# A two-layer graph attention kernel: shorter lookahead and dropped buffers for the gathered rows, four pairs of weighted rows, completing products in three parts

## The chip, the core and the metric

The kernel runs on one core of one Trainium2 chip. The metric is the device time of one execution in microseconds (us); of several runs the median counts. The engines are named as in the profile: PE is TensorE (PEld its weight loads), DVE is VectorE, ACT is ScalarE, POOL is GpSimd, SP is the engine from which most plain DMAs are issued. "SPq" or "POOLq" is an engine's instruction queue.

## What is computed

A graph of 6250 nodes and 100,000 edges, sorted by destination, plus a loop at every node. Two attention layers and a small network are added to x:

```python
def gat_conv(x, src, dst, W, a_src, a_dst, bias, heads):
    n = x.shape[0]
    h = (x @ W).reshape(n, heads, -1)
    alpha_s = (h * a_src[None]).sum(-1)
    alpha_d = (h * a_dst[None]).sum(-1)
    e = jax.nn.leaky_relu(alpha_s[src] + alpha_d[dst], NEG_SLOPE)
    m = jax.ops.segment_max(e, dst, num_segments=n)
    e = jnp.exp(e - m[dst])
    denom = jax.ops.segment_sum(e, dst, num_segments=n)
    alpha = e / (denom[dst] + 1e-16)
    out = jax.ops.segment_sum(h[src] * alpha[:, :, None], dst, num_segments=n)
    return out.reshape(n, -1) + bias

h = jnp.maximum(_layernorm(x, axis=-1), 0.0)
h = jax.nn.relu(gat_conv(h, src, dst, W1, a_src1, a_dst1, b1, HEADS))   # 768 -> 4 heads of 64
h = jax.nn.relu(gat_conv(h, src, dst, W2, a_src2, a_dst2, b2, 1))       # 256 -> 256
h = jax.nn.relu(h @ Wm1 + bm1)
out = x + (h @ Wm2 + bm2)
```

All numbers are float32.

## The kernel before

**Stages.** First the features of all 49 tiles of 128 nodes are computed (lines 519 to 562); each tile's row (features, ones for the denominator, powers of the scores) is kept in SBUF (`kept`) and stored to `table[1]` in memory. Then `layer_edges` runs for layer 1, and while it runs, finished node tiles go through `Node1.steps` to `table[2]`, over the place of `kept`. Then `layer_edges` runs for layer 2, and finished node tiles go through `Node2.steps` to the output.

**Edges.** The edges are cut into tiles of 128, four tiles to a group, 196 groups (NG), and two tiles to a *pair*, the unit of buffers. For every tile GpSimd issues one indirect DMA (line 663) that fetches the 128 source rows out of the table. A pair's rows land in one buffer `G` of the pool `gathered`, which has 20 buffers (line 259). In layer 1 the vector engine makes each edge's weight (lines 741 and 751) and the weighted rows `hw` (line 753) from `G`, and TensorE sums them by destination with a 0/1 matrix `hot` (line 765). In layer 2 the weight is put into the 0/1 matrix (line 748) and TensorE reads `G` itself.

**Order.** The program's order is written out by hand: `layer_edges` walks the groups, and in each group places gathers, `pair(g, 0)`, sums, masks, the steps of node tiles, `pair(g, 1)`. Each engine runs its own part of this order; semaphores join the engines. `gather(g)` is placed AHEAD = 8 groups before `pair(g, 0)`; in the last groups this distance falls to 4 (line 885). From group SHORT = NG - 28 = 168 on, `rows_in(layer, skip)` asks the pool for one more tile at some of the pairs and drops it (lines 320 and 658).

**Pairs fetched soon.** GpSimd has nothing to do in the first stage, so 23 pairs of layer 1 (list SOON) are gathered there, as soon as part of the table is stored: line 357, 46 gathers. Rows that are not there yet are taken as row 0 and masked out. These 23 buffers go to memory (`soon_away`) and come back when their group draws near (`soon_back`, line 368, on SP's queue). The missing rows are completed by a product: `soon_hits` (line 383, vector engine) makes 0/1 matrices, `soon_missing` (line 394, TensorE) multiplies them with the `kept` tiles, 2 to 20 tiles for each of the 46 edge tiles, `soon_out` (line 400, ScalarE) copies the result out of PSUM, and `soon_whole` (line 406, vector engine) adds it into `G`. With `at` the group of such a pair, the product for the first tile is placed in group at-8 and copied out in at-6, that for the second in at-5 and at-3; `soon_whole` stands in group at, before `pair(at, 1)`.

**The seam between the layers.** The first 11 edge tiles of layer 2 are gathered before the last two or three node tiles are finished (`first_rows`, line 334) and completed in the same way (lines 305 and 307).

**Buffers of `hw`.** In layer 1 the weighted rows of a pair use one of 8 buffers (line 640), in layer 2 the weighted 0/1 matrices one of 14.

Of the kernel before, what the change touches and what calls it, by code (L numbers as in the profile page):

```python
# [27 lines left out]
NT = -(-N // P)  # L28
NQ = 4 * NT
TPG = 4  # L30
NG = NQ
# [23 lines left out]
SOON_AT = {2 * g + 1: i for i, g in enumerate(SOON_GROUP)}  # L55
SOON_FROM, SOON_HELD = min(SOON), 16
BARE = 8
SHORT = NG - 28


UP_AT = {4 * u + 11: u for u in range(NU - 16)}
# [10 lines left out]
def kernel(  # L72
# [244 lines left out]
                nc.vector.tensor_tensor(first_i[layer][:, j:j + n], of, ok, ALU.mult)  # L317
                j += n

    def rows_in(layer, skip=False):  # L320

        if skip:
            gp.tile([P, 2, max(TW.values())], F32, name="G")
        return gp.tile([P, 2, max(TW.values())], F32, name="G")[:, :, :TW[layer]]

# [45 lines left out]
    def soon_sources(pool, i):  # L371

        if i < len(SOON):
            soon_of[i] = pool.tile([P, 2 * P], I32, name="soon_of", bufs=2)
            nc.sync.dma_start(soon_of[i], bcast(src_rows, 2 * P, 2 * P * soon_pair[i]))
# [12 lines left out]
    def soon_missing(k):  # L388
        if 0 <= k < 2 * len(SOON):
            there, hit = SOON[k // 2], soon_hit.pop(k)  # L390
            assert not any(T in renewed for T in range(there, NT))
            soon_p[k] = ps.tile([P, TW[1]], F32, name="missing1", tag="n")
            for T in range(there, NT):
                nc.tensor.matmul(soon_p[k], hit[:, T - there], kept[T], start=(T == there),  # L394
                                 stop=(T == NT - 1))

    def soon_out(pool, k):
        if 0 <= k < 2 * len(SOON):
# [235 lines left out]
    def layer_edges(layer, H, node, pre, matched, pre_pool):  # L634
# [2 lines left out]

        C = HID // H
        with tc.tile_pool(name=f"eg{layer}", bufs=6) as eg, \
                tc.tile_pool(name=f"hw{layer}", bufs=8 if layer == 1 else 14) as hwp, \  # L640
                tc.tile_pool(name=f"sum{layer}", bufs=4) as sums, \
                tc.tile_pool(name=f"sm{layer}", bufs=4) as sm:
            G, hot, e_ps, o_ps = {}, {}, {}, {}
# [7 lines left out]
            def gather(g):  # L651
                if not 0 <= g < NG:
                    return
                for t in tiles(g):
                    k = TPG * g + t
                    soon = layer == 1 and k // 2 in SOON_AT
                    if k // 2 not in G:
                        skip = g >= SHORT and k // 2 % (4 if g < SHORT + 9 else 2 if g < SHORT + 18 else 1) == 0
                        G[k // 2] = (soon_back(SOON_AT[k // 2], skip) if soon else
                                     first_G.get(layer, {}).get(k // 2) or rows_in(layer, skip))  # L660
                    if soon or k < FIRST + len(THERE.get(layer, ())):
                        continue
                    nc.gpsimd.indirect_dma_start(  # L663
                        out=G[k // 2][:, k % 2], out_offset=None, in_=table[layer],
                        in_offset=bass.IndirectOffsetOnAxis(ap=src_i[:, k:k + 1], axis=0))
# [66 lines left out]
            def pair(g, p):  # L732

                if 2 * p not in tiles(g):
                    return
                Gp = G.pop(TPG // 2 * g + p)
                e1, e2 = ((Gp[:, :, RW[1]:RW[1] + 4], Gp[:, :, RW[1] + 4:]) if layer == 1 else
                          (Gp[:, :, HID:HID + 1], Gp[:, :, HID + 2:]))
                at = TPG * (g % 4) + 2 * p
                rho, v, w = (e_ps[g // 4][:, at:at + 2, k * H:(k + 1) * H] for k in range(3))  # L740
                nc.vector.tensor_mul(v, e2, rho)  # L741
                if layer == 2:
                    w = sm.tile([P, 2, H], F32, name="w")
                    nc.vector.tensor_max(w, v, e1)  # L744
                    hw = hwp.tile([P, 2, P], F32, name="hw")
                    for t in range(2):
                        k = TPG * g + 2 * p + t
                        nc.vector.tensor_scalar(hw[:, t], iota_ps, dcol[:, k:k + 1], w[:, t],  # L748
                                                ALU.is_equal, ALU.mult)
                else:  # L750
                    nc.vector.tensor_max(w, v, e1)  # L751
                    hw = hwp.tile([P, 2, H, C + 1], F32, name="hw")
                    nc.vector.tensor_mul(  # L753
                        hw, Gp[:, :, :RW[1]].rearrange("p t (h c) -> p t h c", h=H),
                        w.unsqueeze(3).to_broadcast([P, 2, H, C + 1]))
                u = g // 2
                if u not in o_ps:
                    o_ps[u] = ps.tile([P, RW[layer]], F32, name="o_ps", tag="o", bufs=3)
                for t in range(2):
                    k = 2 * p + t  # L760
                    if layer == 2:
                        l, r = hw[:, t], Gp[:, t]
                    else:
                        l, r = hot[g][:, k], hw[:, t].rearrange("p h c -> p (h c)")
                    nc.tensor.matmul(o_ps[u], l, r[:, :RW[layer]], start=(g % 2 == 0 and k == 0),  # L765
                                     stop=(g % 2 == 1 and k == tiles(g)[-1]))
# [4 lines left out]
                    for _ in range(n):  # L771
                        nc.tensor.matmul(idle_ps[0], idle[:, :P], idle, start=True, stop=True)

            done, run, late, idle_ps, begun = {}, {}, [], [], {}

            def take_sum(u):

# [99 lines left out]
            for g in range(NG):  # L877
                t, j = divmod(g, 4)
                if layer == 2 and g >= NG - 2:
                    if g == NG - 2:  # L880
                        last_pairs()
                    continue
                if g == NG - 2:
                    at_end.append(g)
                while gathered < min(NG, g + 1 + min(AHEAD, max(4, SHORT - g))):
                    gather(gathered)
                    gathered += 1
                pair(g, 0)
                if g == NG - 1:
                    pair(g, 1)  # L890
                if g == NG - 2:
                    gather_up(NU - 2)
                advance(g)
                if taken_up(2 * g) is not None:
                    gather_up(taken_up(2 * g))
                if g <= NG - 4:
                    make_hot(g + 1)
                if g in (NG - 4, NG - 3):
                    make_hot(g + 2)
                if j == 0:  # L900
                    if layer == 1:
                        fetch_rows(t + 4)
                    node.prefetch(t)
                    if layer == 2 or t == 0:
                        meet(t + 1)
                    if layer == 1 and t > 0:
                        meet(t + 2)
                elif j == (2 if t < NT - 1 else 1):
                    node.ahead(t)
                elif j % 2 and (layer == 2 or t > 0):  # L910
                    make_mask((g + (11 if layer == 1 else 7)) // 2)
                if layer == 1 and t == 0:
                    for u in ((), (4, 5), (6,), (7,))[j]:
                        make_mask(u)
                    if j == 1:
                        parts_out(1)
                    if j == 2:
                        meet(2)
                if layer == 1:
                    for i, at in enumerate(SOON_GROUP):  # L920
                        for k, hits_at in ((2 * i, at - 10), (2 * i + 1, at - 6)):
                            if g == hits_at + 3 + (k % 2 == 0):
                                soon_out(sm, k)
                            if g == at:
                                soon_whole(G, k)
                            if g == hits_at:
                                soon_hits(pre_pool, k)
                            if g == hits_at + 1 + (k % 2 == 0):
                                soon_missing(k)
                        if g == at - 13:  # L930
                            soon_sources(pre_pool, i)
                if g == NG - 3:
                    idle_ps.append(ps.tile([P, 4 * P], F32, name="idle_ps", tag="parts", bufs=1))
                if g >= NG - 3:
                    stay_warm(3)
                if g < NG - 1:
                    pair(g, 1)
                advance(g, 1)
                if j == 3:
                    if layer == 1:  # L940
                        parts_out(t + 2)
                    join(t + 1)
                if taken_up(2 * g + 1) is not None:
                    gather_up(taken_up(2 * g + 1))
                if NG - 3 <= g < NG - 1:
                    stay_warm(3)
                hot.pop(g, None)
                if layer == 1 and g == NG - 6:
                    first_sources(2)
# [537 lines left out]
```

## Time and profile before

| | us |
|---|---|
| median of 5 runs | 2103.39 (2101.19 to 2106.25) |
| the profiled execution | 2098.68 |
| its span | 2096.8 |

The costliest groups that the change and the prediction touch, from the page (busy us, instructions, mean ns of one):

| line and engine | what | count | busy us | mean ns |
|---|---|---|---|---|
| L663 POOL | gathers of rows | 1507 | 1434.4 | 952 |
| L357 POOL | gathers of the pairs fetched soon | 46 | 44.4 | 964 |
| L753 DVE | weighted rows, layer 1 | 391 | 272.2 | 696 |
| L748 DVE | weighted 0/1 matrices, layer 2 | 782 | 285.0 | 406 |
| L394 PE | completing products | 1028 | 242.1 | 392 |
| L765 PE | sums by destination, layer 1 | 1564 | 454.3 | 426 |
| L765 PE | sums by destination, layer 2 | 1564 | 465.0 | 435 |
| L383 DVE | 0/1 matrices of the completing products | 46 | 75.1 | 1632 |

How to read it: a float32 product of one tile appears as two matmul rows, so 1028 rows at L394 are 514 tile products. The chain that ended last is split by the page as DMA 30%, PE 28%, DVE 18%, issue 13%, POOL 10%; it follows one releaser back at each step and changes engines often. The TensorE clock granted over the span was 0.895 of full speed.

### The profile page before, as it was taken

Reading aid. Unit: us, or ns where it says so; the run is one execution under the profiler, and the core shown is the slowest. Engines: PE = TensorE matmul, PEld = TensorE weight load, DVE = VectorE, ACT = ScalarE, POOL = GpSimd, SP = SyncE. Lnnn points to the kernel's source line nnn. Section 1 sums busy time; section 2 is a strip of 40 time slices with the busy share of each in tenths; the row PEclk is TensorE's granted clock in tenths of the full one; section 3 lists DMA queues with packets and bytes.
Section 4 is the critical chain, followed back from the end, with each engine's and each line's share of the span. In section 5 each row is a group of like instructions: output and inputs, shape, how many; then the busy total and the mean of one; then the engine's idle time right before and its main releaser. Section 6 shows DMA issues by size and latency. Waiting matters only on the chain.

```text
span 2096.8 us, 27028 instructions
## 1 busy us (share of the span) xinstructions
PE 1661.3 (79%) x7727; PEld 1201.2 (57%) x7729; DVE 1417.9 (68%) x4195; ACT 436.7 (21%) x1368; POOL 1526.9 (73%) x1666
## 2 busy tenths in 40 slices
PE   9986878887887888877777777777777777777877
PEld 6874757665665675655545554545555455454544
DVE  7856888887887888888776655555555555555554
ACT  5761111111111111111121111111111111111211
POOL 7067777777777777777777777777777777777774
PEclk9997999989999998999988888888888888888889
DMA  9999666666666666666546455555555555555553
GB/s 346 351 349 323 183 180 188 180 180 186 184 176 184 189 180 186 178 181 182 167 135 224 133 181 177 162 181 167 171 182 157 182 175 164 182 161 177 169 178 108
DMA packets 167330, 400.38 MB, mean 191 GB/s; under 512 B 36631, under 2 KB 54254, under 8 KB 167174
## 3 DMA queue, kind: packets, MB, share of 16 engines
q0 software_dynamic: 75072, 211.10, 37.2%
q1 hardware_dynamic: 90732, 185.99, 24.7%
q10 hardware_dynamic: 1370, 1.48, 0.2%
q8 instruction: 65, 1.06, 0.2%
q14 instruction: 91, 0.75, 0.1%
HBM read 333.87 MB, written 64.56 MB: 190 GB/s over the span
## 4 chain that ended last, share of the span: by engine, by line
DMA 30%; PE 28%; DVE 18%; issue 13%; POOL 10%; ACT 1%; DVEq 0%; SPq 0%; ACTq 0%; POOLq 0%
DMA G<-table,src_i 27%; PE o_ps L765 12%; POOL G L663 10%; PE y_ps L1139 7%; PE h_ps L457 5%; DVE hw L753 4%; DVE soon_hit L383 3%; DVE hot L691 2%; DVE factors L741 2%; DVE hw L748 1%; DVE factors L751 1%; PE y_ps L1078 1%; DVE mask L680 1%; DMA xTt<-in_xT 1%; PE tp L1129 1%
## 5 line engine op out<-in xcount | busy, mean ns | idle before, releaser
L663 POOL DMA_INDIRECT G<-table,src_i x1507 | 1434.4, 952 | 459.1 <-issue 333.6
L765 PE MATMUL o_ps<-G,hw 128*128 128x258 f32 x1564 | 465.0, 435 | 228.7 <-DVE hw L748 227.8
L765 PE MATMUL o_ps<-hw,hot 128*128 128x260 f32 x1564 | 454.3, 426 | 170.5 <-DVE hw L753 155.0
L765 PEld LDWEIGHTS o_ps<-G,hw 128*128 128x128 f32 x1564 | 316.0, 215 | 349.5 <-DVE hw L748 281.1
L741 DVE TENSOR_TENSOR factors<-G,factors 128x8 f32<-128x8 f32 (+1 forms) x782 | 129.2, 165 | 502.6 <-DMA G<-table,src_i 498.4
L765 PEld LDWEIGHTS o_ps<-hw,hot 128*128 128x128 f32 x1564 | 297.8, 204 | 290.5 <-DVE hw L753 222.4
L791 ACT ACTIVATE sum<-acc 32x260 f32<-32x260 f32 (+1 forms) x384 | 160.0, 417 | 1278.8 <-DVE acc L782 1248.6
L753 DVE TENSOR_TENSOR hw<-G,factors 128x520 f32<-128x520 f32 x391 | 272.2, 696 | 39.9 <-DVE factors L751 0.5
L748 DVE TENSOR_SCALAR hw<-iota_ps,dcol,w 128x128 f32<-128x128 f32 x782 | 285.0, 406 | 14.4
L394 PE MATMUL missing<-kept,soon_hit 128*128 128x268 f32 x1028 | 242.1, 392 | 0.0
L394 PEld LDWEIGHTS missing<-kept,soon_hit 128*128 128x128 f32 x1028 | 195.8, 192 | 36.0
L1139 PE MATMUL y_ps<-wm,mT 128*128 128x384 f32 x392 | 202.7, 653 | 0.0
L457 PE MATMUL h_ps<-w,r 128*128 128x264 f32 (+1 forms) x588 | 137.6, 388 | 5.5 <-ACT r L447 5.3
L691 DVE TENSOR_TENSOR hot<-iota_ps,dcol 128x512 f32<-128x512 f32 x196 | 133.6, 682 | 0.0
L457 PEld LDWEIGHTS h_ps<-w,r 128*128 128x128 f32 x588 | 108.4, 191 | 28.0 <-ACT r L447 9.0
L1139 PEld LDWEIGHTS y_ps<-wm,mT 128*128 128x128 f32 x392 | 86.9, 245 | 63.8 <-issue 41.5
L357 POOL DMA_INDIRECT G<-table,soon_i x46 | 44.4, 964 | 74.1 <-DMA xTt<-in_xT 53.9
L782 DVE SCALAR_TENSOR_TENSOR acc<-acc,keep,o_ps 128x260 f32<-128x260 f32 (+1 forms) x192 | 91.3, 476 | 1.8 <-PE o_ps L765 1.8
L751 DVE TENSOR_TENSOR factors<-factors,G 128x8 f32<-128x8 f32 x391 | 68.1, 174 | 13.6 <-DVE factors L741 0.2
L383 DVE TENSOR_TENSOR soon_hit<-soon_of,iota_ps 128x1408 f32<-128x1408 int32 (+18 forms) x46 | 75.1, 1632 | 0.0
L744 DVE TENSOR_TENSOR w<-factors,G 128x2 f32<-128x2 f32 x391 | 62.3, 159 | 13.5 <-DVE factors L741 0.2
L969 ACT ACTIVATE rT<-tp,bT 128x128 f32<-128x128 f32 x196 | 61.1, 363 | 43.3 <-PE tp L963 42.2
(418 smaller groups left out, 1201.6 us busy)
## 6 DMA issues: line engine op xcount, KB each, us to landing
xt<-in_x SPq DMA_DIRECT2D x96, 384.0 KB, 6.0
drow<-dmod_d SPq DMA_DIRECT2D x49, 512.0 KB, 5.6
mask_d<-mask SPq DMA_DIRECT2D x97, 256.0 KB, 2.9
mask<-mask_d SPq DMA_DIRECT2D x97, 256.0 KB, 4.8
G<-table,src_i POOLq DMA_INDIRECT x1507
xTt<-in_xT SPq DMA_DIRECT2D x49, 384.0 KB, 6.7
out<-y SPq DMA_DIRECT2D x48, 384.0 KB, 3.3
table<-kept SPq DMA_DIRECT2D x49, 134.0 KB, 4.6
```

Source lines behind the costliest of these rows:

```text
L383: nc.vector.tensor_tensor(soon_hit[k][:, :m], soon_of[i][:, t * P:(t + 1) * P].unsqueeze(1).to_broadcast([P, m, P]), nid_ps[:, SOON[i]:].u ...
L394: nc.tensor.matmul(soon_p[k], hit[:, T - there], kept[T], start=(T == there), stop=(T == NT - 1))
L457: nc.tensor.matmul(h_ps[:, :n], r[:, k], w1[:, k, :n], start=(k == 0), stop=(k == KI - 1))
L663: nc.gpsimd.indirect_dma_start(out=G[k // 2][:, k % 2], out_offset=None, in_=table[layer], in_offset=bass.IndirectOffsetOnAxis(ap=src_i[:, ...
L691: nc.vector.tensor_tensor(hot[g][:, T[0]:T[0] + n], iota_ps.unsqueeze(1).to_broadcast([P, n, P]), dcol[:, k:k + n].unsqueeze(2).to_broadca ...
L741: nc.vector.tensor_mul(v, e2, rho)
L748: nc.vector.tensor_scalar(hw[:, t], iota_ps, dcol[:, k:k + 1], w[:, t], ALU.is_equal, ALU.mult)
L753: nc.vector.tensor_mul(hw, Gp[:, :, :RW[1]].rearrange("p t (h c) -> p t h c", h=H), w.unsqueeze(3).to_broadcast([P, 2, H, C + 1]))
L765: nc.tensor.matmul(o_ps[u], l, r[:, :RW[layer]], start=(g % 2 == 0 and k == 0), stop=(g % 2 == 1 and k == tiles(g)[-1]))
L782: nc.vector.scalar_tensor_tensor(acc, run[0], keep[:, u % 2:u % 2 + 1], o_ps.pop(u), ALU.mult, ALU.add)
L791: nc.scalar.activation(done[t][r], acc[r], AF.Copy)
L1139: nc.tensor.matmul(y_ps, mT[:, j], wm2[:, j, s * half:(s + 1) * half], start=False, stop=(j == KH - 1))
```

## The change

The numbers that set the distance and the dropping of tiles change, the weighted rows of layer 1 get half the buffers, and `soon_missing` becomes a generator with three parts.

- SHORT is 24. From group 24 on every pair's request drops one tile, and from group 32 on two, in both layers, the 23 pairs that come back from memory among them.
- The distance of `gather(g)` from `pair(g, 0)` is 8 groups up to g = 16, falls by one a group to 4 at g = 20, stays there to g = 26, and is 2 from g = 28 on. `soon_back` is called in `gather`, so for the pairs from group 35 on it moves from group at-8 to group at-2.
- In layer 1 `hw` has 4 buffers instead of 8.
- The products of line 394 are placed in three parts: the first where all stood before, the second after `pair(g, 1)` of the same group, the third in the next group. `soon_out` stays where it was.

```diff
-SHORT = NG - 28
+SHORT = 24
...
-    def rows_in(layer, skip=False):
+    def rows_in(layer, skip=0):
 
-        if skip:
+        for _ in range(skip):
             gp.tile([P, 2, max(TW.values())], F32, name="G")
         return gp.tile([P, 2, max(TW.values())], F32, name="G")[:, :, :TW[layer]]
...
             soon_p[k] = ps.tile([P, TW[1]], F32, name="missing1", tag="n")
-            for T in range(there, NT):
-                nc.tensor.matmul(soon_p[k], hit[:, T - there], kept[T], start=(T == there),
-                                 stop=(T == NT - 1))
+            m = NT - there
+            for part in range(3):
+                for T in range(there + part * m // 3, there + (part + 1) * m // 3):
+                    assert T not in renewed
+                    nc.tensor.matmul(soon_p[k], hit[:, T - there], kept[T], start=(T == there),
+                                     stop=(T == NT - 1))
+                yield
...
-                tc.tile_pool(name=f"hw{layer}", bufs=8 if layer == 1 else 14) as hwp, \
+                tc.tile_pool(name=f"hw{layer}", bufs=4 if layer == 1 else 14) as hwp, \
...
-                        skip = g >= SHORT and k // 2 % (4 if g < SHORT + 9 else 2 if g < SHORT + 18 else 1) == 0
+                        skip = (g >= SHORT) + (g >= SHORT + 8)
...
-            done, run, late, idle_ps, begun = {}, {}, [], [], {}
+            done, run, late, idle_ps, begun, completing = {}, {}, [], [], {}, []
...
-                while gathered < min(NG, g + 1 + min(AHEAD, max(4, SHORT - g))):
+                while gathered < min(NG, g + 1 + min(AHEAD, max(4, SHORT - g), max(2, SHORT + 6 - g))):
                     gather(gathered)
                     gathered += 1
...
                             if g == hits_at + 1 + (k % 2 == 0):
-                                soon_missing(k)
+                                completing.append(soon_missing(k))
                         if g == at - 13:
                             soon_sources(pre_pool, i)
+                    for of in completing[-1:]:
+                        next(of, None)
                 if g == NG - 3:
                     idle_ps.append(ps.tile([P, 4 * P], F32, name="idle_ps", tag="parts", bufs=1))
                 if g >= NG - 3:
                     stay_warm(3)
                 if g < NG - 1:
                     pair(g, 1)
+                for of in completing[-1:]:
+                    next(of, None)
                 advance(g, 1)
```

## The prediction, made before the result was known

> **What bounds the kernel now.** I read the busy times of the page first. TensorE is busy longest, GpSimd next, and neither number says which one sets the end.
>
> ```profile
> span 2096.8 us, 27028 instructions
> ...
> PE 1661.3 (79%) x7727; PEld 1201.2 (57%) x7729; DVE 1417.9 (68%) x4195; ACT 436.7 (21%) x1368; POOL 1526.9 (73%) x1666
> ```
>
> So I split the span by layer (columns: stretch, its length, busy time and instructions of PE, its weight loads, DVE, ACT and POOL, granted clock, DMA share, GB/s).
>
> ```profile
> 165.00:1094.00 929.00, 754.33 (x3656) 571.31 (x3657) 754.61 (x1942) 157.39 (x570) 704.69 (x737) 0.93 0.64 187
> 1110.00:2075.00 965.00, 732.98 (x3308) 494.07 (x3306) 528.31 (x1915) 162.54 (x429) 729.60 (x771) 0.85 0.56 172
> ```
>
> Nobody is full by this. GpSimd's own waits and its order of time decide it. Columns of the waits: total us, times, longest; first stretch 200 to 1090, all its large rows.
>
> ```profile
> POOL G L663 <- issue: 141.7, 465, 0.3
> POOL G L663 <- DVE hw L753: 16.4, 54, 0.3
> POOL G L663 <- DMA G<-table,src_i: 14.6, 48, 0.3
> ```
>
> ```profile
> 101.62 0.95 POOL L357 DMA_INDIRECT G<-table,soon_i  x1 [0.30 <-issue]
> ...
> 1092.34 0.94 POOL L663 DMA_INDIRECT G<-table,src_i  x1 [0.30 <-issue]
> 1093.58 0.94 POOL L334 DMA_INDIRECT G<-table,first_i  x1 [0.30 <-issue]
> 1094.83 1.08 POOL L334 DMA_INDIRECT G<-table,first_i  x1 [0.30 <-issue]
> 1097.92 0.94 POOL L334 DMA_INDIRECT G<-table,first_i  x1 [2.02 <-DVE kept L1022]
> ```
>
> The longest idle time before any L663 gather is 0.3 us, whatever releaser is named; a gather takes 0.95 us and the next starts 1.25 us after it started. The gathers are one unbroken train. Adding it up: first L663 gather at 165.1 us; 736 gathers of layer 1 to 1093.6 (735 steps of 1.25 are 919, the first gather's start to the last's is 927.3, so 8.5 us are gathers that ran long); 11 early gathers of layer 2 to 1109.4, with one stall of 2.02; 771 gathers to the last start at 2073.2 (963.8); then 23.6 us of tail. 165.1 + 928.5 + 15.9 + 963.8 + 23.6 = 2096.9, the span. **GpSimd's gather train sets the end**, at 1.25 us for each of 128 rows. An edit counts only if it changes the number of gathers, the 1.25 us, the start, the 2.02 us, the long gathers or the tail.
>
> One rule of the skill speaks against taking buffers away. The bubble of 0.30 us stands before a gather everywhere, also before the L357 gather at 101.62 us, one of the first that GpSimd issues, into a buffer that nobody had used; so by the rows it is not a wait for a buffer. The Trainium skill, "Perfetto Trace Analysis", section "Optimization Strategy", says that the same gap repeating on the engine that should be saturated can mean too little memory for the next tile; by that rule the 1507 bubbles (459 us in the page) would be what fewer buffers make worse, and I don't follow it, for the row just named.
>
> **The change, part by part.**
>
> *Row buffers and lookahead.* No gather is added or removed: 1507 at L663 before and after. The question is when a gather must wait for the reader of its buffer. I numbered the pairs by their L753 rows (layer 1) and L765 rows (layer 2) in the timeline and counted, at each pair's first gather, how many earlier pairs were not yet read: never more than 4 in layer 1, and from group 24 on never more than 4 in layer 2 (median 3 in both). A pair takes 2.5 us of GpSimd, so with 20 buffers the reserve is 16 pairs, or 40 us; with seven it would be 3 pairs, 7.5 us. From the end of a pair's gathers to the end of its reader the longest is 9.5 us in layer 1 (median 5.2) and 11.6 in layer 2, at its beginning. Cost: 0 either way.
>
> I also doubt that there will be seven. The mechanism is tiles that are asked for and dropped, with no reader and no writer. The kernel before does the same from group 186, one dropped tile a pair, and in its compiled program the gathers there still name the reader of the pair 20 back and the rows still go through all 20 addresses. I take it that dropped tiles take nothing and that the rotation stays at 20. What moves for certain is the program's order: gathers stand 2 groups ahead instead of 8, but GpSimd has nothing else queued in the layers, so its own order is the same.
>
> *The row loads from memory (L368).* These 23 go through SP's queue, and there the place counts. Columns: start, us, issuing queue, line.
>
> ```profile
> 474.12 0.32 SPq L682 DMA_DIRECT2D mask_d<-mask  x1
> 474.49 0.42 SPq L625 DMA_DIRECT2D drow<-dmod_d  x1
> 484.30 0.32 SPq L682 DMA_DIRECT2D mask_d<-mask  x1
> 485.98 0.32 SPq L368 DMA_DIRECT2D G<-soon_d  x1
> 491.71 0.32 SPq L1023 DMA_DIRECT2D table<-kept  x1
> ```
>
> Call `at` the group whose rows are repaired. The rows shown are SP's work of groups at-4 (the store at 474.12), at-3 (`drow`), at-2 (the store at 484.30) and at (485.98, where the next load stands now, and 491.71). The load is moved past six groups of such work: two table stores, three mask stores, two `drow` loads, one `soon_of` load. It would stand between 474.49 and 484.30, and its own wait, for a pair read long before, is over by then, so it would be issued at about 474.9. It lands after 2.7 us (median; 4.6 the longest); the instruction that needs it, L406 of that group, starts at 493.25. Spare: 493.3 - 474.9 - 4.6 = 13.8 us. Cost 0, lower bound 0 (SP's 42.1 us of waiting for L753 before these loads fall away, but SP is not on the path), upper bound below under the rivals.
>
> *Weighted rows, 8 pairs to 4 (L753).* Now the vector engine's L753 of pair n waits for TensorE's last product of pair n-4. Laying L753's rows beside L765's: in three pairs of 391 it started before that, by 0.34, 0.01 and 1.31 us, together 1.7 us. (With three buffers it would be 26 pairs and 41.7 us, with two 67 and 154.) Behind L753 on its engine stand the next pair's factors, the masks, `hot` and `soon_whole`. The cover is the engine's waiting for rows: from 165 to 1094 us L741 waits 105.4 us for gathers. 1.7 against 105.4: cost 0; without cover 1.7.
>
> *Products in three parts (L394).* The same 1028 rows, 242.1 us, all in layer 1. The largest block:
>
> ```profile
> 225.69 2.38 PE L765 MATMUL o_ps<-hw,hot 128*128 128x260 f32 x7
> 227.91 9.20 PE L394 MATMUL missing<-kept,soon_hit 128*128 128x268 f32 x40
> 236.95 1.92 PE L765 MATMUL o_ps<-hw,hot 128*128 128x260 f32 x8
> ```
>
> 40 rows are 20 tiles; a part holds at most 7 tiles, 14 rows of 0.23 us, 3.2 us. So the lag that made those three short waits shrinks, and I expect them to vanish. The last part now ends in the next group, one group before ScalarE's copy L400, which waits 50.3 us already and is waited for by L406 two groups on. If each part's first weight load (0.19 us) is bared, 46 x 2 x 0.19 = 17.5 us of TensorE, which idles 929 - 754 = 175 us in the layer. Cost 0; without cover 17.5.
>
> TensorE's clock was granted at 0.93 in layer 1 with single idle waits of up to 4.2 us (L765 behind L753), and at 0.85 in layer 2. The Trainium skill, "TensorE: Matmul & The Clock Gate", section "What's actually happening", has the array fall to half its clock after an idle window of about 3.4 us and recover only under sustained work; by it, breaking the long blocks could turn layer 1's 754 us into an estimated 754 x 0.93 / 0.5 = 1400, and the layer would be 470 us longer. The row decides: the split moves work within 175 us of idle time and adds none.
>
> *What is left open: the 2.02 us and the long gathers.* At the seam a gather waits for table rows of the last nodes. At best the stall goes: -2.0. At worst all of L753's waits fall there: +1.7. In the span 62 gathers took over 1.0 us, 10.1 us in excess, 8.5 of it in layer 1, mostly beside L406, L680 and L691 on the vector engine. The change keeps these instructions and shifts them; all gone would be -8.5, twice as many +8.5. They are nearest to "as before", so I take 0 for both, and half of each bound, 4.2, for the range.
>
> **Sum**: 2096.8 + 0 = 2096.8 of span; the profiled execution took 2098.68 in all, 1.9 around the span. The median of the runs is 4.7 above that, so I predict the median: 2103.4. Its own range: -2.0 - 4.2 and +1.7 + 4.2, 2097 to 2109.
>
> **Rivals.**
>
> *Slower: the row loads come late.* If SP, which waits up to 17.7 us at a time before a table store (L1023), reaches the moved load more than 13.8 us later than I read, the vector engine stands at L406. It has 105.4 us for 23 loads, 4.6 each, before layer 1 is longer. At 20 us late: (20 - 13.8 - 4.6) x 23 = 37 us, 2140. With seven buffers in truth the 7.5 us of reserve would make it bite earlier, in single lumps. Against it: SP's order above, with 13.8 us spare. For it: SP's queue is in order, and L1023's waits are real. 10%.
>
> *Faster: a smoother layer 1.* Shorter TensorE blocks hold back less, the seam's 2.0 us go and over a quarter of the long gathers with them: 2103.4 - 2.0 - 4.2 = 2097, at most 2093. Against it: nothing removes the vector instructions beside which gathers run long. 9%.
>
> *The buffers don't change* (20 in turn, as argued) is no separate time: 2103.4 as well. Of the 81% for "no change", I give it nine parts in ten.
>
> **How the numbers follow.** 0.2%, 4.2 us, is about what a measurement here can tell from no change. Forecast 81% within it, faster 9%, slower 10%. The range 2097 to 2109 leaves out most of the slower rival, some 8%, and a part of the faster.
>
> **What would show it.** Right: L663 gathers still 1.25 us apart with no wait over 0.3; 1507 of them; L394 in pieces of at most 14 rows; SP's waits at L368 gone; DVE's wait for gathers in layer 1 near 105 us. Wrong: L663 behind L753 or L765 with waits over 0.3 us (then seven buffers are real and too few); L753 behind L765 by more than a few us in total; L406 or L741 behind the load of `soon_d`; a seam stall far from 2 us.

## The result, and the profile after

The changed kernel takes 2103.80 us (median of 24 runs, 2100.61 to 2106.56), the kernel before, run beside it, 2103.58 (44 runs, 2100.76 to 2106.46). The ratio is 0.9998 with a 95% interval of 0.9993 to 1.0004: no change. The forecast was 2103.4.

The page of the profile after, its busy times and the two groups that matter:

```profile
span 2103.1 us, 26974 instructions
...
PE 1659.5 (79%) x7727; PEld 1202.0 (57%) x7729; DVE 1415.0 (67%) x4195; ACT 439.2 (21%) x1368; POOL 1531.5 (73%) x1666
...
L667 POOL DMA_INDIRECT G<-table,src_i x1507 | 1439.3, 955 | 459.5 <-issue 332.0
...
L397 PE MATMUL missing<-kept,soon_hit 128*128 128x268 f32 x1028 | 260.2, 395 | 0.0
```

There are 1507 gathers as before, with the same idle time of 459 us before them, and 1028 matmul rows of completing products as before. By layer (stretch, length, busy time and instructions of PE, its weight loads, DVE, ACT and POOL, granted clock, DMA share, GB/s):

```profile
165.00:1098.00 933.00, 754.32 (x3660) 572.05 (x3662) 752.45 (x1944) 161.14 (x572) 708.23 (x738) 0.93 0.64 186
1115.00:2080.00 965.00, 729.95 (x3303) 493.54 (x3301) 526.44 (x1910) 162.17 (x428) 730.25 (x771) 0.85 0.56 171
```

TensorE's clock is 0.93 and 0.85 in the two layers, as before. GpSimd's waits from 200 to 1090 us (total, times, longest), and its order of time at the seam:

```profile
POOL G L667 <- issue: 144.2, 473, 0.3
POOL G L667 <- DMA G<-table,src_i: 16.2, 53, 0.3
POOL G L667 <- DVE hw L757: 15.0, 49, 0.3
```

```profile
1096.38 0.95 POOL L667 DMA_INDIRECT G<-table,src_i  x1 [0.30 <-issue]
1097.63 0.95 POOL L667 DMA_INDIRECT G<-table,src_i  x1 [0.30 <-issue]
1098.89 0.95 POOL L334 DMA_INDIRECT G<-table,first_i  x1 [0.30 <-DVE all__10488 L1001]
1100.14 0.95 POOL L334 DMA_INDIRECT G<-table,first_i  x1 [0.30 <-issue]
1102.78 0.94 POOL L334 DMA_INDIRECT G<-table,first_i  x1 [1.69 <-DVE kept L1030]
```

The longest wait before a gather inside the layer is still 0.3 us, the train is still unbroken, and the stall at the seam is 1.69 us where it was 2.02. The profiled span is 6.3 us longer than the one before: the first gather of the train starts 1.8 us later (166.8 against 165.1), and the median distance between gathers is 1.254 us in this execution and 1.251 in the one before, over the whole train 4.7 us. Neither is to be put down to the change. Later kernels built on the changed one (seven held pairs, for one) have 1.251 us again, the kernel before with two pairs of weighted rows starts its train at 167.7 us, and the medians of the runs, taken side by side, are equal. The profiled execution of before, 2098.68 us, is faster than each of the 44 runs (lowest 2100.76).

What did change can be seen off the path. TensorE's timeline around the first large completing product, which was one block of 40 rows and 9.20 us:

```profile
230.29 2.87 PE L397 MATMUL missing<-kept,soon_hit 128*128 128x268 f32 x12
233.00 1.04 PE L769 MATMUL o_ps<-hw,hot 128*128 128x260 f32 x4
233.87 3.32 PE L397 MATMUL missing<-kept,soon_hit 128*128 128x268 f32 x14
237.03 1.04 PE L769 MATMUL o_ps<-hw,hot 128*128 128x260 f32 x4
...
238.31 3.41 PE L397 MATMUL missing<-kept,soon_hit 128*128 128x268 f32 x14
```

And SP's queue around one of the moved row loads:

```profile
478.42 0.42 SPq L629 DMA_DIRECT2D drow<-dmod_d  x1
478.94 0.39 SPq L368 DMA_DIRECT2D G<-soon_d  x1
487.46 0.32 SPq L686 DMA_DIRECT2D mask_d<-mask  x1
```

The load stands between the `drow` load and the mask's store; by the packets of the trace the load has landed 5.1 us after its issue. `soon_whole` (L410) of that pair starts at 496.03.

### The profile page after: what moved, and what is told of

Read it like the earlier page. It is cut to its first block, busy times and chain, and to the rows that moved or that the text cites. A ratio compares the mean times of both kernels' runs of the same rounds, so it can differ in the third digit from the quotient of the medians.

```text
span 2103.1 us, 26974 instructions
## 1 busy us (share of the span) xinstructions
PE 1659.5 (79%) x7727; PEld 1202.0 (57%) x7729; DVE 1415.0 (67%) x4195; ACT 439.2 (21%) x1368; POOL 1531.5 (73%) x1666
## 4 chain that ended last, share of the span: by engine, by line
PE 28%; DMA 27%; DVE 23%; issue 13%; POOL 8%; DVEq 0%; ACT 0%; SPq 0%; ACTq 0%; POOLq 0%
DMA G<-table,src_i 24%; PE o_ps L769 13%; POOL G L667 8%; PE y_ps L1147 7%; DVE hw L757 5%; PE h_ps L461 4%; DVE hot L695 3%; DVE soon_hit L383 3%; DVE factors L755 2%; DVE factors L745 2%; DVE hw L752 1%; DVE mask L684 1%; PE y_ps L1086 1%; DMA xt<-in_x 1%; DVE acc L786 1%
## 5 line engine op out<-in xcount | busy, mean ns | idle before, releaser
L397 PE MATMUL missing<-kept,soon_hit 128*128 128x268 f32 x1028 | 260.2, 395 | 0.0
```

## The experiments

The kernel before ran beside each set of them on the same chip, and the ratios are to it. On the chip of the first four, called the pausing chip here, TensorE stands again and again without a wait that the profile shows (numbers in the last section), and the kernel before itself took 2521.79 us there (17 runs, 2515.94 to 2531.74). So three of their questions were asked again on other chips, where it took 2100.67 and 2099.84. In the compiled programs two things could be read without a run: in the changed kernel every gather still waits for the reader of the pair 20 back and the rows still go through 20 addresses; and the changed kernel with the dropped tiles left out becomes the same program, 0 of 21598 instructions differing. "About seven pairs in turn" doesn't happen.

**Seven pairs in truth.** Thirteen buffers are taken at group 34 and given back at group 192, so that the gathers' waits name the pair seven back.

```diff
-                        skip = (g >= SHORT) + (g >= SHORT + 8)
+                        skip = 0
...
+                if g == SHORT + 10:
+                    for _ in range(13):
+                        held.append(gp.tile([P, 2, max(TW.values())], F32, name="held", tag="G"))
+                        nc.vector.memset(held[-1][:, 0, 0:1], 0.0)
+                if g == NG - 4:
+                    for of in held:
+                        nc.vector.memset(of[:, 0, 0:1], 0.0)
```

> The changed kernel, but with seven row buffers in truth: instead of dropping tiles, 13 of the 20 buffers are held by a tile that is written at group 34 and again at group 192 of each layer, so that a gather in between must wait for the reader of the pair seven back. Theory (GpSimd's unbroken train of gathers sets the end, and at most 5 pairs are unread when a gather is issued): no wait over 0.3 us before a gather, 2103.6 us within 0.2%, 2099.4 to 2107.8. Rival (buffers bind, and the change cost nothing only because the dropped tiles take no buffer): waits of GpSimd for L757 or L769 over 0.3 us, and more than 2108 us.

On the pausing chip 2524.31 against 2521.79 us, ratio 1.0011 (0.9996 to 1.0027). Again, on another chip:

> The changed kernel with thirteen of the twenty row buffers really held from group 34 to group 192 of both layers, so that seven pairs are used in turn (the same kernel as the first experiment, again, on another chip). My theory, that the buffers are far more than the train of gathers needs: no wait of a gather for a reader over 0.3 us beyond the ones of before, ratio 1.000 within 0.002. Rival, that seven pairs make gathers wait for the pair seven back: from the distances between issue and read in the trace of after, at most a few waits of about 0.4 us each (2.8 us in all at five buffers), so a rival that is over 4 us slower (ratio over 1.002) would need readers that are late by more than that trace shows.

2097.24 against 2099.84 us, ratio 0.9987 (0.9978 to 0.9997). The interval lies just below 1; no trace shows why. GpSimd's waits with seven real pairs, in layer 1 and then in layer 2:

```profile
POOL G L667 <- DVE hw L757: 17.7, 58, 0.3
```

```profile
POOL G L667 <- PE o_ps L769: 25.0, 82, 0.3
```

No wait before a gather inside the layers is over 0.3 us: from group 34 on seven pairs are enough, and the changed kernel would take the same time if its dropped tiles did what they seem to.

**Four pairs.** Sixteen buffers held, until group 188, and gathers one group ahead instead of two. The lines are against the kernel with seven pairs.

```diff
-                    for _ in range(13):
+                    for _ in range(16):
...
-                if g == NG - 4:
+                if g == NG - 8:
...
-                while gathered < min(NG, g + 1 + min(AHEAD, max(4, SHORT - g), max(2, SHORT + 6 - g))):
+                while gathered < min(NG, g + 1 + (2 if g >= NG - 3 else min(AHEAD, max(4, SHORT - g), max(1, SHORT + 6 - g)))):
```

> As the run with seven held, but 16 buffers are held, four are in turn, and gathers stand one group ahead instead of two. Theory (the reserve is the number of buffers less the pairs unread at issue): in the trace of the changed kernel the pair four back is still unread at 57 pairs of layer 1 (52 us in sum) and 52 of layer 2 (49 us), so the train breaks; about four fifths of the groups are held, which gives 40 to 100 us more, 2145 to 2205 us, with GpSimd's waits for L757 and L769 showing it. Rival (buffers don't matter at any number, something else paces the gathers): 2104 us.

On the pausing chip 2566.48 us, ratio 1.0169 (1.0139 to 1.0198). Again:

> The changed kernel with sixteen of the twenty row buffers held and gathers issued one group ahead, so that four pairs are used in turn from group 34 on (the same kernel as the second experiment, again, on another chip). My theory, that only below about five pairs the wait for a reader comes onto the train: some 50 us of first-order stall in each layer from the distances in the trace of after (52.3 and 48.7 us), so 40 to 100 us longer, ratio 1.02 to 1.05, with waits of gathers for VectorE's products of several tenths of a microsecond. Rival, that buffers never matter here, because a wait of one gather is caught up by the next: within 0.2%.

2165.66 against 2099.84 us, ratio 1.0324 (1.0308 to 1.0340), 65.8 us longer. GpSimd's order of time in layer 2:

```profile
1347.53 0.95 POOL L667 DMA_INDIRECT G<-table,src_i  x1 [0.32 <-PE o_ps L769]
1348.78 0.94 POOL L667 DMA_INDIRECT G<-table,src_i  x1 [0.30 <-issue]
1352.38 0.94 POOL L667 DMA_INDIRECT G<-table,src_i  x1 [2.66 <-PE o_ps L769]
1353.63 0.95 POOL L667 DMA_INDIRECT G<-table,src_i  x1 [0.30 <-issue]
```

Here the train is broken, and a broken train isn't caught up: the distances between gathers exceed 1.251 us by 20.3 us in layer 1 (8.7 in the kernel before) and by 52.2 in layer 2 (1.5 before). So between seven pairs and four, with the shorter lookahead, the buffers begin to count. The shorter lookahead alone wasn't run, but of the 69 waits that are longer than the usual 0.3 us, 83 us in all, 64 with 80 us name a reader of the rows. The estimate from issue and read in the trace of after, about 50 us in each layer, was right in layer 2 (50.7 us more than in the kernel before) and over four times too much in layer 1 (11.6 us more).

**Two pairs of weighted rows**, in the changed kernel (`bufs=4` to `bufs=2`) and in the kernel before (`bufs=8` to `bufs=2`).

> The changed kernel with two pairs of weighted rows in layer 1 instead of four. Theory (VectorE has 110 us of waiting for rows in layer 1 that hide what it waits for TensorE): from the changed kernel's rows, L757 would have started before the product two pairs back was done in 34 pairs, 33.7 us in sum, all hidden: 2103.6 us within 0.2%, VectorE's waits for gathers down by 20 to 40 us. Rival (VectorE's waits come through one for one): 2137 us.

> The kernel before (completing products in one piece, 20 row buffers, old lookahead) with two pairs of weighted rows in layer 1 instead of eight. Theory: from the rows of the kernel before, L753 would start too early in 67 pairs, 154 us in sum, against 105 us of waiting for rows: from 0 to 49 us more, 2104 to 2153 us, and clearly more waits of L753 behind L765 than with the products in three parts. Rival one (one for one): 2258 us. Rival two (TensorE's blocks never hold VectorE): 2104 us with no such waits.

On the pausing chip 2548.07 us (1.0105, 1.0079 to 1.0130) and 2551.07 us (1.0110, 1.0081 to 1.0140), which would speak for a cost; the changed kernel with two pairs wasn't run elsewhere. The kernel before with two buffers, again:

> Again the kernel before with two pairs of weighted rows in layer 1 instead of eight. Theory: L753 would start too early in 67 pairs, 154 us in sum, against 105 us of VectorE's waiting for rows: from 0 to 49 us more, 2104 to 2153 us. Rival one (one for one): 2258 us. Rival two (TensorE's blocks never hold VectorE): 2104 us with no waits of L753 for L765.

2100.34 against 2100.67 us, ratio 0.9999 (0.9990 to 1.0008). VectorE's waits in layer 1:

```profile
DVE hw L753 <- PE o_ps L765: 99.9, 29, 7.2
...
DVE factors L741 <- DMA G<-table,src_i: 6.1, 7, 1.3
```

99.9 us of waiting for TensorE appear, and the waiting for gathers falls from 105.4 to 6.1. The sum is 106.0: one wait has taken the other's place, to a microsecond, and the time hasn't moved. The count from the rows, 154 us, was too high.

Of the reserve 6.1 us are left. On the pausing chip there is none to begin with: in the traces of seven held pairs and of both kernels with two pairs of weighted rows VectorE never waits for a gather in layer 1. What TensorE makes it wait comes out at the seam, where GpSimd's first gather of layer 2's rows stands as follows, first with seven held pairs (and four of weighted rows), then in the changed kernel with two of weighted rows:

```profile
1328.16 1.15 POOL L334 DMA_INDIRECT G<-table,first_i  x1 [8.65 <-DVE acc L804]
```

```profile
1338.69 1.12 POOL L334 DMA_INDIRECT G<-table,first_i  x1 [34.06 <-DVE acc L804]
```

In the kernel before with two pairs it is 34.01 us. The 25.4 us between these stalls are about what lies between the medians, 23.8 and 26.8 us. So the same edit costs 1% there because nothing covers it. (Of the kernel before with its eight pairs there is no trace on that chip.)

**Fewer gathers.** In each layer 39 gathers are replaced by plain loads of the table's first 128 rows (other rows than the reference's).

```diff
+                    if t == 1 and g % 4 == 1 and 32 <= g <= 188:
+                        nc.sync.dma_start(G[k // 2][:, 1], table[layer][:P])
+                        continue
```

> The changed kernel with 39 gathers of each layer (the second tile of groups 33, 37, ... 185) taken from GpSimd: SP loads the table's first 128 rows into their place, the same bytes, so the sums of these tiles are of other rows. Theory (GpSimd's train sets the end, 1.25 us a gather, and VectorE and TensorE have the reserve to follow): 78 x 1.25 = 98 us less, 2006 us, 1.25 us between the gathers that remain. Rival (the path runs through the landing of the rows and the engines behind it, as the chain of waits seems to say): 2090 to 2104 us.

2000.73 us, ratio 0.9524 (0.9510 to 0.9539): 99.9 us less, for 78 gathers of 1.25 us (97.5). The gathers that remain are still 1.251 us apart (median):

```profile
L670 POOL DMA_INDIRECT G<-table,src_i x1429 | 1359.3, 951 | 435.4 <-issue 286.5
```

SP issues 78 more loads; VectorE, TensorE and ScalarE have as many instructions as before. That GpSimd's train sets the end is shown.

**The row loads at their use.** The moved load is put where `soon_whole` needs it.

```diff
-        G = rows_in(1, skip)
-        nc.sync.dma_start(G.rearrange("p t c -> p (t c)"), soon_d[i])
-        return G
+        return rows_in(1, skip)
...
+                                if k % 2 == 0:
+                                    nc.sync.dma_start(G[soon_pair[i]].rearrange("p t c -> p (t c)"), soon_d[i])
```

> The changed kernel with the 23 loads of the pairs fetched soon issued as late as can be, in the group that uses them, directly before VectorE's L410. Theory (VectorE's stalls hide behind its 110 us of waiting for rows in layer 1): VectorE stands 3 to 5 us at each of 23 loads, 70 to 115 us in sum, its waiting for gathers falls to between 0 and 40 us, and the time stays within 0.2% or grows by at most 10 us: 2101 to 2114 us. Rival (a late load comes through one for one): 2175 to 2220 us.

2132.33 us, ratio 1.0146 (1.0131 to 1.0162), 31.7 us longer. VectorE's waits up to 1100 us, and GpSimd at the seam:

```profile
DVE G L408 <- DMA G<-soon_d: 125.7, 22, 7.4
...
DVE factors L743 <- DMA G<-table,src_i: 5.2, 4, 1.8
```

```profile
1102.59 0.94 POOL L665 DMA_INDIRECT G<-table,src_i  x1 [0.30 <-issue]
1132.86 1.03 POOL L334 DMA_INDIRECT G<-table,first_i  x1 [29.34 <-DVE acc L802]
```

5.7 us a load, where 3 to 5 were expected. By the packets of the trace such a load lands 3.6 to 6.5 us after its issue (median 4.9); at its old place in the kernel before the median is 2.5. VectorE's waiting for gathers pays for the first hundred; the rest makes it late, and late VectorE shows at the seam (29.34 us), where GpSimd needs the last node tiles. The other distances of over 1.6 us between gathers add 10.6.

**More pairs fetched soon.** By these runs VectorE has a hundred microseconds of room in layer 1 and GpSimd has none. So four more pairs (21 to 24 tiles missing) are fetched in the first stage, 27 instead of 23; the room in SBUF for the wider `soon_hit` comes from the `hw` buffers that the change gave up.

```diff
-SOON = [NT - m for m in (11, 20, 2, 19, 11, 18, 3, 18, 4, 17, 4, 16, 5, 15, 10, 15, 7, 14, 13, 12, 9, 8,
-                         6)]
-SOON_GROUP = [8 * i + 11 for i in range(len(SOON))]
+SOON = [NT - m for m in (11, 24, 20, 2, 19, 11, 23, 18, 3, 18, 4, 22, 17, 4, 16, 5, 21, 15, 10, 15, 7, 14, 13, 12, 9, 8, 6)]
+SOON_GROUP = [11 + 176 * i // (len(SOON) - 1) for i in range(len(SOON))]
```

> The changed kernel with 27 instead of 23 pairs fetched in the first stage: four more, with 21 to 24 tiles each to be completed, spread over the groups 11 to 187; their 0/1 matrices are larger and fit because the weighted rows have four buffers. The first gather can start when 25 instead of 29 tiles of the table are stored. Theory (only the start, the number and the pace of GpSimd's gathers count): the train starts some 11 us earlier and everything behind it shifts by as much, 2093 us (2090 to 2097), though TensorE gets 8 x 22.5 x 0.46 = 83 us more in layer 1 of the 175 us it idles, and VectorE some 28 us of 110. Rival (TensorE and VectorE are near enough to full that the added products cost more than the earlier start brings): 2104 to 2130 us, with GpSimd's stall at the seam larger than 2 us.

2098.25 against 2100.67 us, ratio 0.9992 (0.9983 to 1.0001): 2.4 us, not the 10 expected. The train starts earlier but has holes, where a gather needs a tile of the table that isn't computed yet:

```profile
146.51 0.94 POOL L356 DMA_INDIRECT G<-table,soon_i  x1 [4.12 <-DVE mv L431]
...
150.61 0.94 POOL L356 DMA_INDIRECT G<-table,soon_i  x1 [1.91 <-DVE cent L448]
```

Two of them are 4.12 and 1.91 us long. The first gather comes 10.6 us earlier than before (89.6 against 100.2 us), the 47th only 4.5 (160.6 against 165.1). The profiled execution is the fastest of its eleven (2092.84 us), so these views show more of a gain than the median has. VectorE's waiting for gathers in layer 1 is down to 59.6 us.

**Fuller still.** Eight more pairs than the kernel before, 31, four of them chosen to fill those holes.

```diff
...
+SOON = [NT - m for m in (15, 14, 18, 11, 18, 11, 19, 10, 20, 10, 21, 8, 21, 5, 22, 4, 24, 4, 23, 3, 20, 2, 17, 16, 15, 13, 12, 10, 9, 7, 6)]
+SOON_GROUP = [11 + 176 * i // (len(SOON) - 1) for i in range(len(SOON))]
```

> The changed kernel with 31 instead of 23 pairs gathered in the first stage (eight more: 24, 23, 22, 21, 21, 20, 10 and 10 missing tiles), placed so that the gaps that the 27-pair run still had in the first stage's gathers (6 us before its 47th gather, 5.4 us of it at the tiles with 9 and 8 missing) are filled. My theory, that the end of the train sets the time and VectorE still has room (59.6 us of its waiting for gathers were left with 27 pairs, and these four take some 31 us more): 5 to 12 us shorter than before, ratio 0.994 to 0.998. Rival, that the work added to VectorE and TensorE in layer 1 now makes the gathers wait there: not shorter than before, with waits of gathers for VectorE's weighted rows over 0.3 us in layer 1.

2090.39 us (5 runs, 2089.84 to 2095.68) against 2099.84, ratio 0.9958 (0.9944 to 0.9972): 9.4 us faster than the kernel before, the fastest here that sums the reference's rows. The profile shows only part of it, for the profiled execution is the slowest of the five (2095.68; the others 2089.84 to 2091.01). Its 63rd gather starts at 182.6 us, 2.6 earlier than the 63rd of the kernel before, and its first stage still has holes, the longest a wait of 3.75 us; where the rest of the 9.4 us comes from no trace shows. Then the same with each completing product in one block again:

```diff
-            for part in range(3):
-                for T in range(there + part * m // 3, there + (part + 1) * m // 3):
+            for part in range(1):
+                for T in range(there, NT):
```

> The same 31 pairs, with the completing products of a row in one block again instead of three parts; the rest of the change stays. My theory, that the three parts only move TensorE's work inside its own slack: the same time as with three parts within 0.2%, VectorE's waits for TensorE in layer 1 (for the output sums, with the four buffers of weighted rows) longer in a single case, up to 9 us, but not the end. Rival, that with four buffers and more rows a block holds up the weighted rows long enough to reach the gathers: 5 to 20 us slower than with three parts.

2099.20 us (11 runs, 2094.35 to 2103.10), ratio 0.9999 (0.9990 to 1.0008). My theory falls and the rival holds: with 31 pairs the three parts are worth 8.8 us (the difference of the medians; the two intervals don't touch), nearly the whole gain. The views say how. TensorE and then VectorE in the kernel with blocks:

```profile
653.05 13.01 PE L396 MATMUL missing<-kept,soon_hit 128*128 128x268 f32 x48
665.89 1.92 PE L768 MATMUL o_ps<-hw,hot 128*128 128x260 f32 x8
```

```profile
661.41 0.17 DVE L754 TENSOR_TENSOR factors<-factors,G 128x8 f32<-128x8 f32 x1
666.97 0.70 DVE L756 TENSOR_TENSOR hw<-G,factors 128x520 f32<-128x520 f32 x1 [5.39 <-PE o_ps L768]
```

A block of 48 rows holds TensorE for 13.01 us; VectorE fills its four buffers of weighted rows, runs out, and stands for 5.39 us. With three parts TensorE at about the same place:

```profile
654.76 2.87 PE L396 MATMUL missing<-kept,soon_hit 128*128 128x268 f32 x12
657.47 1.04 PE L768 MATMUL o_ps<-hw,hot 128*128 128x260 f32 x4
...
659.22 3.77 PE L396 MATMUL missing<-kept,soon_hit 128*128 128x268 f32 x16
662.83 3.67 PE L768 MATMUL o_ps<-hw,hot 128*128 128x260 f32 x16
```

From 600 to 900 us VectorE's waits for TensorE are these, in blocks and then in parts:

```profile
DVE hw L756 <- PE o_ps L768: 30.0, 11, 5.4
```

```profile
DVE hw L756 <- PE o_ps L768: 20.2, 12, 3.1
```

In that stretch VectorE never waits for a gather in either kernel, so it is behind the train and has nothing to pay with; from 900 us to 1100 it catches up in parts (it waits 5.8 us for gathers again) but not in blocks (it doesn't wait for one). The bill comes at the seam, at GpSimd's first gather of layer 2's rows, first in blocks, then in parts:

```profile
1089.07 0.94 POOL L666 DMA_INDIRECT G<-table,src_i  x1 [0.30 <-issue]
1099.06 0.95 POOL L333 DMA_INDIRECT G<-table,first_i  x1 [9.04 <-DVE factors L754]
```

```profile
1091.64 0.95 POOL L666 DMA_INDIRECT G<-table,src_i  x1 [0.30 <-issue]
1093.09 1.17 POOL L333 DMA_INDIRECT G<-table,first_i  x1 [0.51 <-DVE rden L1013]
1094.57 0.95 POOL L333 DMA_INDIRECT G<-table,first_i  x1 [0.30 <-issue]
1096.93 0.94 POOL L333 DMA_INDIRECT G<-table,first_i  x1 [1.42 <-DVE kept L1029]
```

The two kernels' longest distances at the seam are 9.98 and 2.37 us, 7.6 us apart. No other stretch of the two traces differs as much. The profiled spans differ by 5.2 us (2099.1 and 2093.9), because the execution with parts also began the dense part of its train 1.8 us later (its 63rd gather at 182.6, in blocks at 180.8 us); how the 8.8 us between the medians divide up beyond the seam isn't shown.

## Why the prediction was right, step by step

- *The gather train sets the end.* Shown by the fewer gathers: 99.9 us for 78 of them, 1.28 each where the step is 1.25.
- *Row buffers, 0 either way.* Shown twice: the dropped tiles leave the program as it is, and seven held pairs cost nothing (0.9987). The reserve had been read as "never more than 4 pairs unread"; in the trace of after it is up to 5 in layer 1, which seven still hold and four don't (65.8 us). That the 0.30 us bubble isn't a wait for a buffer holds too: it is 0.30 with 20 pairs, with seven and with four. The Trainium skill, "Perfetto Trace Analysis", section "Optimization Strategy", reads a repeating gap as a possible lack of memory for the next tile; the measurement decides against it here.
- *Row loads past six groups of SP's work, 13.8 us to spare.* The order on SP was as read: the load was issued at 478.94, directly behind `drow`, and SP's waits at these loads fell from 42.1 us to 3.3. The time to land was mis-sized. The prediction took it from the old place, 2.7 us and 4.6 the longest. At the new place, by the packets of the trace of after, the 20 moved loads land 3.8 to 7.3 us after their issue, median 6.0, and their first packet starts up to 4.0 us after it, where it was at most 2.1 at the old place. The `drow` load before them is of 512 KB; whether that is the reason wasn't tested. The load shown had 12.0 us to spare, the worst of the 20 had 11.2: the cost stays 0, since the spare was large enough for the error. The slower rival's mechanism is real where the loads do come late: 31.7 us. The rival's own formula, lateness beyond 4.6 us a load, gives (5.7 - 4.6) x 23 = 25 us for it. What the prediction didn't name is the place where it comes out: mostly the seam.
- *Weighted rows 8 to 4, at most 1.7 us.* In layer 1 of after VectorE doesn't wait for TensorE at this line at all, so not even the 1.7 us came; it waits 109.8 us for gathers. That the cover named, 105.4 us, would have paid is shown by the kernel before with two buffers, where it paid 99.9.
- *Three parts, 0.* Right for this kernel, the parts are of at most 14 rows and 3.4 us. None of the 17.5 us of bared weight loads shows: the products' own busy time is 260.2 us where it was 242.1, but TensorE's in layer 1 is 754.32 where it was 754.33. That blocks do cost time where the cover is nearly used up is shown at 31 pairs: VectorE's waiting for gathers in layer 1 is down to 16.9 us there, and the same split is worth 8.8 us. The price "without cover" that I gave, up to 17.5 us lost to bared weight loads, looked at TensorE only and had the wrong sign; what a block without cover costs is VectorE's time. The split undone in the changed kernel with its 23 pairs wasn't run, so that it was the cover which made it free here is likely, not shown.
- *The clock.* 0.93 and 0.85 before and after. With 31 pairs in parts it is 0.96 and 0.84. These are means of two values: the clock records of the traces hold 1.0 and 0.5 and nothing else, and in layer 1 some 106 us before and 113 after are at half, in stretches of 3.4 to 10.2 us.
- *Seam and long gathers, 0 with 4.2 us of range.* The stall is 1.69 where it was 2.02; 66 gathers over 1.0 us with 10.7 us in excess, where 62 had 10.1. (Of the 10.1 the gathers of layer 1 themselves hold 7.9; the prediction's 8.5 is what the layer's steps exceed 1.25 us by.)
- *The faster rival*, a smoother layer 1, didn't come: VectorE's instructions, beside which gathers run long, are the same.

In the prediction the landing time of the moved loads was off. In the experiments sizes were off too: a late load costs 5.7 us, not 3 to 5, and four more pairs gave 2.4 us, not 10, largely because the first stage's tiles come too slowly to keep GpSimd's earlier gathers dense.

## What to carry to other kernels

When one engine's unbroken train sets the end, price every edit by the waits that cover it, and write down how much cover there is: here 105 us of VectorE's waiting for rows hid all of the 99.9 us that two pairs of weighted rows cost, and all but 31.7 of the 125.7 us that late loads cost. The change itself drew nothing from it, 109.8 us are left. An edit that is worth nothing today may be needed by the next one: the three parts moved no time in this change, but with more rows fetched in the idle first stage they carried 8.8 us. Before arguing about a buffer count, look in the compiled program whether the count changes at all.

## What was not expected of the hardware

The pace of the train differs between executions: the median distance is 1.251 us in most profiles and 1.254 in that of after and in three of the four from the pausing chip, which over 1563 steps is 4.7 us, more than most edits here are worth. So one profile against one profile says nothing below 5 us, and the ratio of many runs is needed.

On the pausing chip TensorE stands without a wait that the profile shows. In the trace of seven held pairs there, from 200 to 2450 us, 108 of its idle times over 1.5 us end with nothing released just before, 255 us in all; in the traces of after and of the kernel before with two pairs on another chip none does. The other engines wait behind it, in part for something that the profile can't name ("remote"); VectorE's, from 200 to 1090 us:

```profile
DVE hw L757 <- remote: 166.5, 38, 8.8
```

The granted clock of that run was 0.815 over the span, and the kernel before took 1.20 times as long as elsewhere (2521.79 against 2103.58). Why TensorE stands there stays open.
